# A four-layer graph network on one core: layer 0 moved beside the scatter of the edge records, with the edge counts taken from its own matmuls

## The chip, the cores and the metric

The kernel runs on one core of a Trainium2 chip. The core has a tensor engine (PE, whose weight loads are shown as PEld), a vector engine (VectorE, shown as DVE), a scalar engine (ScalarE, shown as ACT), GpSimd (shown as POOL) and SyncE (SP), which only issues DMAs here. ACT and POOL issue DMAs too. Each engine works off its own instructions in order and waits on semaphores. The metric is device time of one execution in microseconds (us); smaller is better.

## The reference, cut to what matters

There are 12500 nodes with 16 features and 412500 edges (200000 random pairs in both directions, and a loop at each node), sorted by target `dst`. Four layers follow one another, each with a residual and a layer norm over the 16 features:

```python
x = _layernorm(x + _L0_gnn_ref(x, src, dst, edge_type_8, ...))      # one 16x16 matrix per edge type, then a gated unit
x = _layernorm(x + _L1_gnn_ref(x, edge_attr_16, ..., src, dst))     # a matrix from each edge's 16 attributes
x = _layernorm(x + _L2_gnn_ref(x, ..., edge_index, edge_type_8))    # twice: sums over edge types, each divided by its count
x = _layernorm(x + _L3_gnn_ref(x, edge_index, ...))                 # reflections, weighted by 1/sqrt(degree) of both ends
```

Layer 0 sums `emb[type(e)] @ x[src(e)]` over the edges `e` of each target. Layer 2 needs, for every target and every one of 8 types, `1 / max(count, 1)`, where the count is the number of edges of that type into the target. Layer 3 needs `1 / sqrt(degree)`, where a node's degree counts it as source and as target.

## The kernel before, in words

**Places.** `find_places` (L804) computes for each edge its place in a table `rb` in DRAM. The table has 100 blocks of 125 targets (and one spare block); a block holds 39 tiles of 128 edges, grouped in 13 cells by the block of the source: `cells_of` (L794) gives a cell 3 tiles, or 2 or 4. A record is 20 floats: node number of the target within its block, the same of the source, the low three bits of the source's block, the type, and the 16 attributes. Unused places hold codes that match nothing. `find_places` also sets a flag if the edges are not sorted or a cell overflows, and then `general_path` runs instead of `sorted_path`; with this input it doesn't.

**Scatter and counts.** `sorted_path` (L930) first turns the codes by PE transposes and DVE arithmetic (L1102 to L1134). Then, in chunks of 32 tiles (`CT`), SP loads the attributes into a buffer `rec` (L1153), ACT writes the four codes beside them (L1155), and POOL issues one indirect DMA for each of the 3223 tiles of 128 edges, called a put here (L1158). The puts are declared free of dependencies on each other. In the same loop each tile is counted: DVE makes four one-hot rows by comparisons (L1147), and PE multiplies them to `cnt_ps` and `deg_ps` (L1172, L1176). The code orders PE, DVE, ACT and SP by hand there (`manual_schedule`: each engine issues in the order in which the program is written); POOL's order is the scheduler's. At the end the counts become `inv`, a tile in SBUF of all inverse counts, and `dis`, the inverse roots of the degrees (L1181 to L1194).

**Layers.** After that the node features are loaded and turned, and `table`, three bf16 parts of them, is made (n0, L1401 to L1409). `by_type` runs layer 0 (called e0, L1410) and, later, both halves of layer 2 (e2a, L1543, and e2b, L1548); between them stands layer 1 (e1, L1455), and layer 3 (e3) is last. Each of these five runs over all 1300 cells in a written-out software pipeline (`Layer.run`, L1292): in step i the work is `prepare`, delayed functions, then stage `rows` of cell i, `products` of cell i-1, and `sums` of cell i-2. In `by_type`:

- `rows`: three bf16 matmuls gather the source rows (L1265); DVE masks them with the low bits (L1267); POOL makes a one-hot row of targets for each tile (L1276).
- `products`: PE folds the masked rows (L1346); DVE multiplies by the type's one-hot `w8` (L1348).
- `sums`: PE adds a block's messages by type and target into `acc` (L1372). With `mean` (e2a, e2b) the block's inverse counts are spread by DVE (L1363), turned by PE (L1365) and copied by ACT (L1369), and multiply the sums (L1382). Later one matmul applies the types' matrices (L1388).

`start_of` (L1306) places the preparation: the record load of block d+2 in cell 3 of block d (L1222), the turning of its codes in cell 6, only in e0 (L1229 to L1233), the broadcast loads of block d+1 in cell 0 (L1237, L1239), and the one-hots of its source columns in cells 8 to 10 (L1246).

Of the kernel before, what the change touches and what calls it, by code (L numbers as in the profile page):

```python
# [8 lines left out]
F32 = mybir.dt.float32  # L9
# [8 lines left out]
P = 128  # L18
D = 16
R = 8  # L20
# [22 lines left out]
CT = 32  # L43
ENG = mybir.EngineType
# [759 lines left out]
def find_places(tc, a, rb, addr_d, flag):  # L804
# [3 lines left out]
    with tc.tile_pool(name="nat", bufs=1) as nat, tc.tile_pool(name="natp", bufs=1, space=PSUM) as psum:  # L808
# [46 lines left out]
        bads = small("bads", [P, 2])  # L855
        nc.vector.scalar_tensor_tensor(
            junk, prv_i, 1.0, dst_i, op0=OP.mult, op1=OP.is_gt, accum_out=bads[:, 0:1]
        )
        keep = big("keep")
# [63 lines left out]
        bad_ps = psum.tile([1, 2], F32, name="bad_ps")  # L923
# [7 lines left out]
def sorted_path(ctx: ExitStack, tc: tile.TileContext, a: dict, out: bass.AP, rb: bass.AP, addr_d: bass.AP):  # L931
# [43 lines left out]

    def column(name, w, j=0):
        to = const.tile([P, 1], F32, name=name)
        nc.sync.dma_start(to, w[:, j : j + 1])
        return to
# [34 lines left out]
    inv = state.tile([P, NDB, R], F32, name="inv")  # L1014
# [72 lines left out]

    with tc.tile_pool(name="sort", bufs=1) as sort, tc.tile_pool(name="sortp", bufs=1, space=PSUM) as psum:
        at = sort.tile([P, NT], I32, name="at")
        js, ds = sort.tile([P, NT], F32, name="js"), sort.tile([P, NT], F32, name="ds")  # L1090
        jd, dr = sort.tile([P, NT], F32, name="jd"), sort.tile([P, NT], F32, name="dr")
        lo, ty = sort.tile([P, NT], BF16, name="lo"), sort.tile([P, NT], BF16, name="ty")

        def by_tile(to, rows):

            for q in range(0, NQ, 4):
                n = min(4, NQ - q)
                tp = psum.tile([P, 4, P], F32, name="tp", bufs=2)
                for k in range(n):
                    nc.tensor.transpose(tp[:, k, :], rows[:, q + k, :], ident)  # L1100
                w = min(n * P, NT - q * P)
                nc.scalar.copy(to[:, q * P : q * P + w], tp.rearrange("p b f -> p (b f)")[:, :w])  # L1102

        with tc.tile_pool(name="code", bufs=1) as work:
            rows = work.tile([P, NQ, P], F32, name="rows_f")
            nc.vector.memset(rows, 0.0)
            whole = NT // P
            nc.sync.dma_start(
                rows[:, :whole, :], addr_d[: whole * P * P].rearrange("(q r i) -> r q i", r=P, i=P)
            )  # L1110
            nc.scalar.dma_start(
                rows[: NT - whole * P, whole, :], addr_d[whole * P * P :].rearrange("(r i) -> r i", i=P)
            )
            by_tile(at, rows)
            for to, name in ((js, "src"), (jd, "dst"), (ty, "edge_type_8")):
                rows_i = work.tile([P, NQ, P], I32, name="rows_i")
                nc.sync.dma_start(rows_i, a[name].rearrange("(q r i) -> r q i", r=P, i=P))
                rows = work.tile([P, NQ, P], F32, name="rows_f")
                nc.vector.tensor_copy(rows, rows_i)
                by_tile(to, rows)  # L1120
            q = work.tile([P, NT], I32, name="q")
            fix = work.tile([P, NT], F32, name="fix")
            for j, b in ((js, ds), (jd, dr)):
                nc.vector.tensor_scalar(q, j, 1049.0, None, op0=OP.mult)
                nc.vector.tensor_scalar(q, q, 17, None, op0=OP.logical_shift_right)
                nc.vector.tensor_copy(b, q)
                nc.vector.scalar_tensor_tensor(j, b, -float(NB), j, op0=OP.mult, op1=OP.add)
                nc.vector.tensor_scalar(fix, j, 0.0, None, op0=OP.is_lt)
                nc.vector.tensor_sub(b, b, fix)
                nc.vector.scalar_tensor_tensor(j, fix, float(NB), j, op0=OP.mult, op1=OP.add)  # L1130
# [860 lines left out]
```

## Time and profile before

| | |
|---|---|
| time, median of 3 runs (lowest to highest) | 22925.8 us (22896.29 to 22970.97) |
| the profiled execution: its own time | 22977.63 us |
| its span | 22975.7 us |
| mean granted PE clock | 0.919 |
| places and code columns, up to the first put | 0 to 594 us |
| scatter (puts), counting beside it up to 3229 us | 594 to 5266 us |
| layer 0 (n0 and e0) | 5266 to 7985 us |
| layer 1 (e1) | 8056 to 11530 us |
| e2a, then e2b | 11530 to 14139, 14139 to 16754 us |
| layer 3 and output | 16754 to 22975 us |

The profile's page begins with the busy time of each engine, then cuts the span into 40 equal slices (one digit each, tenths of the slice in which the engine was busy; PEclk is the clock that was granted to PE, in tenths of full speed). The chain that ended last is followed back from the last instruction, and its shares are given by engine and line. Groups of instructions show the engine, the operation, output and inputs by the program's names, shapes, the number, busy time and mean duration in ns, and the idle time before them with what ended it. A table of windows gives for each stretch its length, the busy time (and instructions) of each engine, the granted clock, the DMA share and GB/s. A timeline line has start, duration, engine, line and operation. A line of waits has the engine and line that waited, what it waited for, the total in us, the number and the longest.

### The profile page before, as it was taken

The numbers are of one execution on the slowest core, as the hardware profiler recorded it, in microseconds if no ns is written. First come the engines' busy times: TensorE is split into PE (matmuls) and PEld (weight loads), VectorE is DVE, ScalarE is ACT, GpSimd is POOL, SyncE is SP. The second block draws the span as 40 slices with busy tenths as digits, with TensorE's granted clock in tenths as the row PEclk, the third lists the DMA queues.
The fourth block names the chain that finished last, engine by engine and source line by source line (L and its number), as shares of the span: only waits on it lengthen the run. The fifth ranks groups of instructions, "written<-read, shape, count | busy, mean of one in ns | idle before, by whom it ended". The sixth has DMA issues, their size and how long they took to land.

```text
span 22975.7 us, 392949 instructions
## 1 busy us (share of the span) xinstructions
PE 18801.4 (82%) x144828; PEld 16753.0 (73%) x144830; DVE 15165.8 (66%) x35158; ACT 2307.5 (10%) x8260; POOL 16182.6 (70%) x22749
## 2 busy tenths in 40 slices
PE   0666640007999999999989999999989999999998
PEld 0444430006888878888888888888879999999998
DVE  7999960004656666666666666666657777777776
ACT  0000000000000001111100000000022222222222
POOL 2788877777988866666689998999934545554444
PEclk9999985558989999999999999999979999999998
DMA  2100011112323244444433332333323333333333
GB/s 94 13 12 12 12 13 15 15 15 75 92 82 86 78 143 139 141 142 142 131 86 91 90 92 81 90 92 90 92 75 97 106 97 105 104 102 103 99 104 80
DMA packets 1173120, 1910.62 MB, mean 83 GB/s; under 512 B 578330, under 2 KB 962721, under 8 KB 1094017
## 3 DMA queue, kind: packets, MB, share of 16 engines
q1 hardware_dynamic: 1050430, 1830.86, 28.4%
q0 software_dynamic: 103136, 33.21, 1.0%
q8 instruction: 1154, 18.91, 0.4%
q10 hardware_dynamic: 17627, 21.31, 0.3%
q14 instruction: 773, 6.33, 0.1%
HBM read 1557.01 MB, written 327.89 MB: 82 GB/s over the span
## 4 chain that ended last, share of the span: by engine, by line
PE 63%; POOL 19%; DMA 6%; issue 5%; DVE 5%; another core or an unknown queue 0%; ACT 0%; SPq 0%; POOLq 0%; ACTq 0%; DVEq 0%
POOL rb L1158 15%; PE g L1265 12%; PE acc L1372 10%; PE acc L1488 8%; PE x L1346 8%; DMA rec<-rb 5%; PE acc_s L1835 4%; PE hid_ps L1720 4%; POOL target L1276 4%; PE acc_s L1828 3%; PE side L1728 3%; PE x L1471 3%; PE edge_ps L1689 3%; PE acc_s L1619 1%; DMA rb<-rec,at 1%
## 5 line engine op out<-in xcount | busy, mean ns | idle before, releaser
L1276 POOL TENSOR_SCALAR target<-iota_f,rec 128x125 f32<-128x125 f32 x15600 | 9376.8, 623 | 2079.9 <-PE acc L1488 904.0
L1267 DVE SCALAR_TENSOR_TENSOR masked<-lo,part_lo,g 128x384 f32<-128x384 uint8 (+2 forms) x6500 | 3985.0, 613 | 3612.2 <-PE g L1265 3524.3
L1816 POOL TENSOR_SCALAR from_s<-iota_f,js_e 128x125 f32<-128x125 f32 x3900 | 2954.1, 773 | 3233.3 <-PE acc_s L1835 2991.8
L1265 PE MATMUL g<-oh,table 125*128 125x384 bf16 (+2 forms) x19500 | 4359.2, 332 | 169.6 <-DVE oh L1246 103.9
L1158 POOL DMA_INDIRECT rb<-rec,at x3223 | 3690.4, 1145 | 1074.5 <-issue 982.0
L1372 PE MATMUL acc<-target,pr 128*128 128x125 f32 x23400 | 3632.2, 292 | 0.0
L1346 PEld LDWEIGHTS x<-fold,masked 128*128 128x128 f32 x23400 | 3197.0, 196 | 280.1 <-issue 22.1
L1372 PEld LDWEIGHTS acc<-target,pr 128*128 128x128 f32 x23400 | 3012.6, 197 | 0.4
L1346 PE MATMUL x<-fold,masked 128*128 128x16 f32 x23400 | 2948.2, 252 | 0.0
L1265 PEld LDWEIGHTS <-table 125*128 125x128 bf16 x19500 | 1970.8, 106 | 880.7 <-issue 212.6
L1172 PE MATMUL cnt_ps<-in_col,in_row 128*125 128x400 bf16 x6446 | 1607.7, 330 | 915.4 <-DVE in_col L1147 915.4
L1348 DVE TENSOR_TENSOR pr<-x,w 128x384 f32<-128x384 f32 (+2 forms) x3900 | 2170.7, 557 | 134.0 <-PE x L1346 108.0
L1488 PE MATMUL acc<-pr,target 128*125 128x272 f32 x7800 | 2106.6, 406 | 0.0
L1172 PEld LDWEIGHTS <-in_row 128*125 128x125 bf16 x6446 | 857.5, 133 | 1262.2 <-issue 643.5
L1045 PE MATMUL tp<-ident,x_rows 125*128 125x125 f32 x13 | 5.9, 465 | 2052.1 <-DMA x_rows<-in_x 2050.1
L1488 PEld LDWEIGHTS acc<-pr,target 128*125 128x125 f32 x7800 | 1364.8, 188 | 216.9 <-issue 0.3
L1045 PEld LDWEIGHTS tp<-ident,x_rows 125*128 125x128 f32 x13 | 2.4, 182 | 2055.6 <-issue 2043.0
L1474 DVE TENSOR_TENSOR pr<-x,rec 128x768 f32<-128x768 f32 (+2 forms) x1300 | 1244.8, 958 | 257.1 <-ACT pr L1473 251.9
L1147 DVE TENSOR_SCALAR in_col<-iota_h,dr 128x800 bf16<-128x800 f16 x3223 | 1322.9, 410 | 0.0
L1835 PE MATMUL acc_s<-placed,from_s 128*125 128x128 f32 x7800 | 1249.1, 299 | 53.8 <-DVE acc_s L1833 51.4
L1192 DVE RECIPROCAL dis<-root 128x104 f32<-128x104 f32 x1 | 0.8, 803 | 1921.7 <-ACT root L1191 1921.7
L1720 PE MATMUL hid_ps<-x_t,w_h 96*128 96x128 f32 (+2 forms) x7800 | 1188.1, 292 | 0.0
(303 smaller groups left out, 25808.5 us busy)
## 6 DMA issues: line engine op xcount, KB each, us to landing
hi<-hi_d SPq DMA_DIRECT2D x400, 1218.8 KB
lo<-lo_d SPq DMA_DIRECT2D x500, 624.0 KB
to_d<-target SPq DMA_DIRECT2D x1108, 187.5 KB
target<-to_d SPq DMA_DIRECT2D x1108, 187.5 KB
rec<-rb SPq DMA_DIRECT2D x500, 390.0 KB
oh<-hi_d SPq DMA_DIRECT2D x100, 1218.8 KB
to_t<-jd_d SPq DMA_DIRECT2D x100, 1218.8 KB
rb<-rec,at POOLq DMA_INDIRECT x3223, 2.5
```

What stands on the lines that cost most here:

```text
L1158: put = nc.gpsimd.indirect_dma_start(out=rb, out_offset=bass.IndirectOffsetOnAxis(ap=at[:, t : t + 1], axis=0), in_=rec[:, k, :], in_offse ...
L1172: nc.tensor.matmul(cnt_ps[:NB, h, :NC2], in_row, in_col[:, h * NC2 : (h + 1) * NC2], start=False, stop=False, skip_group_check=True,)
L1265: nc.tensor.matmul(g[:, :w], tab[:NB, s, k, :], self.oh[d][:NB, cols], start=k == 0, stop=k == 2)
L1267: nc.vector.scalar_tensor_tensor(m[:, :w], self.lo[d][:, cols], part_lo, g[:, :w], op0=OP.is_equal, op1=OP.mult)
L1276: nc.gpsimd.tensor_scalar(oh[:, k, :], iota_f[:, :NB], self.rec[d][:, t + k, code : code + 1], None, op0=OP.is_equal)
L1346: nc.tensor.matmul(x[:, k, :D], m[:, k * P : (k + 1) * P], fold, start=True, stop=True)
L1348: nc.vector.tensor_tensor(pr[:, :n], x[:, :n, None, :D].to_broadcast([P, n, R, D]), layer.w8[d][:, t : t + n, :, None].to_broadcast([P, n, ...
L1372: nc.tensor.matmul(acc[:, :NB], pr[:, k].rearrange("p r f -> p (r f)"), oh[:, k, :], start=t + k == 0, stop=t + k == TB - 1,)
L1488: nc.tensor.matmul(acc[:NB, :WE], oh[:, k, :], pr[:, k, :], start=t + k == 0, stop=t + k == TB - 1)
L1720: nc.tensor.matmul(ps[:, k * P : (k + 1) * P], w_h[rows, k, :], x_t[rows], start=True, stop=True)
L1816: nc.gpsimd.tensor_scalar(oh[:, k, :], iota_f[:, :NB], js_e[d][:, t + k : t + k + 1], None, op0=OP.is_equal)
L1835: nc.tensor.matmul(acc_s[:NB, s // 4, s % 4, :], oh[:, k, :], placed[:, k].rearrange("p l f -> p (l f)"), start=False, stop=False, skip_gr ...
```

## The change

Layer 0 runs inside the scatter's loop. The diff, cut to its core:

```diff
+EB = 4125
+WAYS = 8
+SLACK = 2048
...
+        nc.gpsimd.iota(q, pattern=[[1, NT]], base=0, channel_multiplier=NT)
+        nc.vector.tensor_copy(x1, q)
+        nc.vector.scalar_tensor_tensor(x1, d, -float(EB), x1, op0=OP.mult, op1=OP.add)
+        nc.vector.tensor_scalar(x1, x1, float(EB + SLACK), None, op0=OP.is_ge)
+        nc.vector.tensor_reduce(bads[:, 2:3], x1, AX.X, OP.add)
...
-                for t in range(t0, t0 + n):
-                    in_row = one_hot("in_row", jd[:, t : t + 1], NB)
-                    in_col = one_hot("in_col", dr[:, t : t + 1], NDB * R)
-                    out_row = one_hot("out_row", js[:, t : t + 1], NB)
-                    out_col = one_hot("out_col", ds[:, t : t + 1], NDB)
...
-            nc.sync.dma_start(self.rec[d], rb_v[d])
+            load = nc.sync.dma_start(self.rec[d], rb_v[d])
+            tc.add_to_no_dep_group("records", getattr(load, "ins", load))
...
-            tp = self.psum.tile([P, 4, P], F32, name="codes_t", bufs=1)
+            tp = self.psum.tile([P, 512], F32, name="g", bufs=2).rearrange("p (b c) -> p b c", b=4)
...
+                for k in range(n):
+                    rec = layer.rec[d][:, t + k, :]
+                    nc.vector.tensor_scalar(oh[:, k, :], iota_f[:, :NB], rec[:, 0:1], None, op0=OP.is_equal)
+                    nc.scalar.activation(away[:, k, :], iota_f[:, :NB], AF.Abs, bias=rec[:, 1:2], scale=-1.0)
+                source = work.tile([P, 4, NB], BF16, name="source", bufs=4)
+                nc.scalar.activation(source[:, :n], away[:, :n], AF.Relu, bias=1.0, scale=-1.0)
+                for _ in range(2):
+                    nc.tensor.matmul(
+                        deg_ps[:, P:], zeros[:, :P], zeros[:, P:], start=False, stop=False, skip_group_check=True
+                    )
...
-                if mean and s == NS - 3:
...
+                if mean and s == 2:
...
-                    nc.scalar.copy(state_["inv", d], ps[:, :NB])
+                    nc.sync.dma_start(state_["inv", d], inv_d[d])
...
+                    if first:
...
+                        nc.tensor.matmul(
+                            acc[:R, P : P + NB], layer.w8[d][:, t + k, :], oh[:, k, :].bitcast(BF16)[:, 1::2],
+                            start=False, stop=t + k == TB - 1, skip_group_check=True,
+                        )
+                        nc.tensor.matmul(
+                            deg_ps[:NB, s * LO : (s + 1) * LO], source[:, k, :], layer.lo8[d][:, t + k, :],
+                            start=False, stop=False, skip_group_check=True,
+                        )
...
+                def count():
+                    nc.tensor.matmul(
+                        deg_ps[:NB, d : d + 1], cnt, ones8, start=False, stop=False, skip_group_check=True
+                    )
+                    ps = psum.tile([P, 4, 32], F32, name="x", bufs=2).rearrange("p k c -> p (k c)")
+                    nc.tensor.matmul(ps[:, :NB], spread8, cnt, start=True, stop=True)
+                    inv = work.tile([P, NB], F32, name="inv_t", bufs=2)
+                    nc.vector.tensor_scalar(inv, ps[:, :NB], 1.0, None, op0=OP.max)
+                    nc.vector.reciprocal(inv, inv)
+                    nc.sync.dma_start(inv_d[d], inv)
...
+            def fed(layer, steps):
...
+                chunk(0)
+                chunk(1)
+                i = 0
+                for t in range(NT + WAYS):
+                    if t % CT == 0:
+                        chunk(t // CT + 2)
+                    put(t)
+                    while i < len(all_cells) and (EB * max(3.0, 3 + (i - 3) / NS) + SLACK) / P + WAYS < t:
+                        next(steps)
+                        i += 1
+                for _ in steps:
+                    pass
```

In words:

- `fed` writes the program so that after put t those steps of e0 stand whose records can't lie behind put t-8, as long as no edge of a block stands more than 2048 edges behind its mean place. `find_places` checks that in addition (four DVE passes and an iota). A block takes 4125/128 = 32.2 puts. Eight puts to the spare block are added at the end. The attributes and codes of a chunk are asked for two chunks ahead, in four buffers instead of three.
- The separate counting is gone, with the columns that only it used. In e0 each tile gets two thin matmuls more: `w8` times the targets' one-hots, which counts edges by type and target into a free part of `acc`, and the sources' one-hots times the one-hots of the low bits (`lo8`), which counts degrees. The sources' one-hots come from ACT (Abs, then Relu). Two matmuls of zeros with 384 columns stand in each cell.
- In e0 the targets' one-hots are made by DVE instead of POOL; in the other layers POOL keeps them. `w8` is bf16 in all `by_type` layers.
- After each block of e0 its counts are spread over the features by PE, limited to 1 and inverted by DVE, and stored in DRAM (`inv_d`, 64 KB). e2a and e2b load that in cell 2 of a block instead of copying, turning and copying from `inv`.
- The load and turning of the node features and `table` (n0) stand ahead of the code columns, since e0 needs them from the start.

## Prediction

> **What bounds the kernel now.** I first read the slices of the span on the page: the tensor engine (PE) stands idle in slices 7 to 9 while GpSimd (POOL) works on, and everything behind them is a row of nines.
>
> ```profile
> PE   0666640007999999999989999999989999999998
> ...
> DVE  7999960004656666666666666666657777777776
> ...
> POOL 2788877777988866666689998999934545554444
> PEclk9999985558989999999999999999979999999998
> ...
> POOL rb L1158 15%; PE g L1265 12%; PE acc L1372 10%; PE acc L1488 8%; PE x L1346 8%; DMA rec<-rb 5%; PE acc_s L1835 4%; PE hid_ps L1720 4%; POOL target L1276 4%; PE acc_s L1828 3%; PE side L1728 3%; PE x L1471 3%; PE edge_ps L1689 3%; PE acc_s L1619 1%; DMA rb<-rec,at 1%
> ```
>
> The last line is from the chain that ended last: 15% of the span is the scatter, L1158. Its 3223 puts are one chain on POOL from 594.0 to 5265.5 us. Then I cut the span at the stage borders (first instructions of each stage, from the per-line view): busy time of PE, weight load, DVE, ACT, POOL, then the granted clock.
>
> ```profile
> 594.00:3175.00 2581.00, 1711.61 (x9460) 1260.70 (x9458) 2581.00 (x12612) 29.99 (x196) 2100.67 (x1577) 1.00 0.10 12
> 3175.00:5266.00 2091.00, 36.84 (x206) 27.03 (x204) 63.44 (x275) 31.59 (x198) 1589.31 (x1647) 0.51 0.12 14
> 5266.00:7984.00 2718.00, 2586.70 (x20011) 2355.74 (x20011) 1702.80 (x3003) 92.67 (x417) 2349.12 (x3901) 0.94 0.32 87
> ...
> 11530.00:14139.00 2609.00, 2486.25 (x19921) 2281.42 (x19921) 1750.98 (x3207) 37.37 (x123) 2358.22 (x3900) 0.98 0.33 89
> ```
>
> Row 1: scatter beside counting, DVE full. Row 2: counting is done, scatter alone, PE at half clock with nothing to do. Row 3: layer 0 (e0), bounded by PE (95% busy). Row 4: e2a, the same. So 4672 us hang on POOL, then 2718 us on PE, one after the other. The put itself is seen at two prices; timeline of POOL in both stretches:
>
> ```profile
> 4000.17 0.96 POOL L1158 DMA_INDIRECT rb<-rec,at  x1 [0.30 <-issue]
> ...
> 2001.70 1.34 POOL L1158 DMA_INDIRECT rb<-rec,at  x1 [0.30 <-issue]
> ```
>
> Busy 0.96 us and 0.30 between: one put per 1.263 us beside an idle DVE (3.79 us for three at 4000.17); 1.34 and 0.30, one per 1.637 us (2581/1577) beside a DVE that does nothing but L1147's comparisons. That difference of 0.374 us is the disputed price.
>
> **The change, part by part.**
>
> *1. First put (+34 us).* Loading x and making the table now comes ahead: 27 us (5267.8, first x load issued, to 5295.0, first record load issued). Four more DVE passes over 128x3223 in the check (1.8, 3.5, 1.8, 3.5 us by the rows of L1126, L1127, L1128, L1129) and an iota, 3.3 us (L951: 0.81 us for 800 columns, times 4): 14. Two passes go with the counting's columns (L1129, L1134 of dst, 3.5 each): -7. First put at 594 + 34 = 628.
>
> *2. The puts.* 3223, and 8 to the spare block: 3231 at a price r. It lies between 1.263 and 1.637 by the two rows. DVE's work per block of targets in e0: masked 7.97 us (L1267, 3985.0/500), pr 7.24 (L1348, 2170.7/300), the 39 target one-hots that leave POOL for DVE, 39 x 0.2 = 7.8 (L1147 starts one of 125 columns every 0.16; L953, 128 columns of f32, lasts 0.21), column one-hots 3 x 0.70 (L1246), w8 and lo8 1.0 (L1253), maximum and reciprocal 1.2 (L1192: 0.80 for 104 columns): 27.3 us. Of these 11.1 (one-hots, maximum, reciprocal) resemble L1147's. A block is 4125 edges, 32.2 puts, about 43.7 us. I take the surcharge as proportional: 0.374 x 11.1/43.7 = 0.095, r = 1.358, 3231 x 1.358 = 4388 us. Last put at 5016. I keep both ends: 4081 to 5289.
>
> *3. Does e0 fit below it?* PE: today (7984 - 5326)/100 = 26.6 us a block, of which 1.3 waits. Added: 39 counting matmuls of 125 columns and 39 degree matmuls of 8, and 26 of zeros with 384 (two a cell). The nearest rows, in layer 3:
>
> ```profile
> 20011.42 0.29 PE L1691 MATMUL edge_ps<-x_parts,to_t 125*128 125x96 bf16 x3
> 20011.55 0.23 PE L1696 MATMUL side<-dis_tab,oh 125*128 125x24 bf16 x3
> 20011.63 0.81 PE L1828 MATMUL acc_s<-msg,target 128*125 128x16 f32 x6
> ```
>
> Starts tell the price: three of 96 columns in 0.13 us, three of 24 in 0.08. So 0.06 and 0.03 each: 3.5 us; those of zeros 0.163 as in L1265 (0.49 for three): 4.2. Together 33 us. DVE 27.3. ACT: per cell three activations of 0.26 (L1380, 128x125) and one of at most 0.58 (L1722, 384 columns), 17.7 a block, with codes, counts and record columns 21. All are under 43.7, so the puts stay the bound, and the counting's 12612 DVE instructions (2581 us, row 1) vanish. Target one-hots on POOL, 24.3 us a block, would have stood in the puts' queue; moved, they don't. On SP each block's record load waits for the put before it, and behind it stand column stores and broadcasts (1219 and 624 KB), the inverse's store and the next chunk's attributes. Chunks are asked for two ahead, 64 puts or 87 us; a block's queue is at most 44 us late if PE keeps pace. If that cover went, POOL would wait for ACT and SP: rival A.
>
> *4. What is late next.* The program lets a block start some 3.5 blocks behind its last possible edge: 35 cells remain after the last put, 35 x 33/13 = 89 us, plus load and broadcast of the last block: 115 (89 to 230 if half-clocked). e0 ends at 5016 + 115 = 5131; layer 0's gates today start at 7985 (L1421). Gain 2854.
>
> *5. e2a and e2b.* The turned inverse (L1363, L1365, L1369) becomes a 64 KB load.
>
> ```profile
> PEld x L1365 <- PE x L1346: 85.4, 86, 1.0
> PE x L1365 <- DVE by_f L1363: 79.5, 86, 0.9
> ```
>
> PE waits 0.94 us a block for the copy (188.1/200 over both layers) and issues two f32 passes, 0.22: 200 x 1.16 = 232 us. POOL's targets (three start in 1.75 us, 22.8 a block) and the load, asked for ten cells ahead, are not later. Ends: 0 (something else is late at once) to 290 (35 short half-clock stretches go too). I take 230, since PE is busy 95% around that wait.
>
> *6. bf16 w8, a shared PSUM ring for the transposed codes:* 0, the first lies beside PE, the second can at worst hold PE for ACT's two further copies of 0.26 a block (L1232): 0 to +52, inside the tail's and r's bounds, since e0 is not the bound.
>
> **Sum** against the profiled execution (22977.6, span 22975.7): 22977.6 - 2854 - 230 = 19894. That execution lies 52 us above the median 22925.8; with the same cut the median becomes 19842, say **19850**.
>
> [...]
>
> [...] PE around a wait of 1.47 us for records in e0:
>
> ```profile
> 5660.00:5690.70 30.70, 29.68 (x244) 1.00 0.35 97
> 5690.70:5694.20 3.50, 2.03 (x17) 1.00 0.03 10
> 5694.20:5718.10 23.90, 23.90 (x106) 0.50 0.27 80
> 5718.10:5745.00 26.90, 26.90 (x222) 1.00 0.23 62
> ```
>
> One such wait brought 23.9 us at half clock, and 106 instructions where 190 would go. [...] By the row PE, ready after 33 of 43.7 us, will wait, drop, fall behind, not wait, and recover: it needs a mean clock of 0.76 and lags less than the 87 us of cover. Counting ran at clock 1.00 with PE 66% busy (row 1), with gaps of 0.3 us.
>
> **Rivals.**
> A. *PE stays at half clock.* For: the row above. Against: row 1, and a PE that is behind has no gaps. 66 us a block; e0 would end at 628 + 164 (121 puts ahead of the first cell) + 6600 = 7392, 2261 later: 22,100. 13%.
> B. *No overlap:* each record load waits for all puts. For: one tensor, rb, is written and read, and only puts are declared free of each other. Against: the wait is for puts issued before the load. Then 628 + 3231 x 1.263 + 3300 = 8009, and with e2's gain 22,720. 5%.
> C. *Slower: the put's price explodes.* If a put that loses to DVE waits for a whole train of three one-hots, twice, it costs 1.263 + 2 x 0.6 = 2.46 us, e0 ends at 628 + 7948 + 115 = 8691, time 23,400. It decides from r = (7985 + 230 - 628 - 115)/3231 = 2.31. For: DVE did slow puts. Against: a DVE without a gap cost only 0.374. 5%.
>
> **Numbers.** Forecast 77%: own range 19,450 (r 1.263, e2 290, short tail) to 20,980 (r 1.637, e2 0). Range 19,450 to 21,300, which takes in blocks of up to some 57 us from A. The measurement tells 0.3% (69 us) from no change. Faster 0.94, same 0.01 (B with a small extra wait), slower 0.05.
>
> **What would show it.** Puts from about 628 at 1.30 to 1.45 us apart throughout, e0's matmuls from about 800, layer 0's gates near 5130; PE 75 to 95% busy there at a clock above 0.75; no wait of PE for an inverse in e2, blocks of 25 us. Wrong if POOL waits for ACT's record columns by more than some us per chunk (A), if e0 starts behind the last put (B), or if puts are over 1.64 apart (C).

## The result and the profile after

The changed kernel takes 24,767.0 us (median of 4 executions, 24,735.9 to 24,807.6), the kernel before 22,931.4 (22,896.3 to 22,971.0): a ratio of 1.0801 with a 95% interval of 1.0777 to 1.0825. The forecast was 19,850. The profiled execution took 24,807.6 us (span 24,805.8).

| stage border (us from the span's start) | before | forecast | after |
|---|---|---|---|
| first put | 594.0 | 628 | 621.9 |
| last put | 5265.5 | 5016 | 9830.2 |
| layer 0's gates (its gated unit's first product, behind all its sums) | 7985.3 | 5131 | 10183.6 |
| from the gates to the end | 14990.4 | 14760 | 14622.2 |

So everything behind layer 0 gained 368 us, and layer 0 with its scatter, which was to gain 2854, lost 2198.

The page of the changed kernel, first the slices (busy tenths, granted clock), then the chain that ended last, then the put's row in the costliest groups (busy us, mean ns of one, idle before and its releaser):

```profile
PE   0478777776777777999999999999998999999998
...
POOL 2433333323333332366666899999993554545544
PEclk9555555556565555899999999999997999999998
...
PE 79%; another core or an unknown queue 10%; DVE 5%; issue 3%; POOL 1%; DMA 1%; ACT 0%; SPq 0%; ACTq 0%; DVEq 0%; POOLq 0%
...
L1454 POOL DMA_INDIRECT rb<-rec,at x3223 | 3102.2, 963 | 6159.0 <-ACT rec L1445 4244.4
```

TensorE now works in the scatter, but at a clock of 0.5 to 0.6 from slice 2 to slice 16. GpSimd, which was to set the pace, is three tenths busy. A put still lasts 0.96 us, so its price didn't rise; GpSimd stands idle for 6159 us, mostly until ScalarE has filled the columns of a chunk of 32 tiles. And 10% of the chain, some 2480 us, has no releaser that the profile knows. That last item is the odd one, so I cut one period into windows: busy PE, weight load, DVE, ACT, POOL, then the clock, DMA share, GB/s.

```profile
622.00:9830.00 9208.00, 6725.46 (x28912) 4753.62 (x28912) 2460.72 (x6765) 1841.36 (x5764) 3108.80 (x3230) 0.55 0.13 32
4017.00:4039.00 22.00, 21.66 (x84) 15.25 (x83) 4.83 (x14) 4.85 (x16) 16.33 (x17) 0.50 0.05 7
4039.00:4063.00 24.00, 3.97 (x14) 2.34 (x14) 1.07 (x2) 0.11 (x1) 14.40 (x15) 0.50 0.05 7
4063.00:4110.00 47.00, 46.37 (x186) 32.91 (x186) 17.83 (x50) 12.56 (x38) 0.00 (x0) 0.50 0.22 57
9860.00:9960.00 100.00, 100.00 (x412) 71.62 (x412) 34.11 (x94) 25.18 (x76) 0.00 (x0) 0.52 0.08 25
13700.00:18600.00 4900.00, 4823.08 (x39476) 4436.11 (x39476) 3478.99 (x6231) 29.48 (x61) 4715.92 (x7800) 0.99 0.37 97
```

Row 2: a burst of 32 puts begins at 4017.6 and TensorE works beside it. Row 3: in the second half of the same burst TensorE issues 14 matmuls in 24 us, VectorE 2 instructions, ScalarE 1. Row 4: the burst is over, GpSimd waits, TensorE is full, at half clock. Row 5: all puts are done and TensorE is 100% busy without one gap, and still at 0.52. Row 6 lies over layer 2's two passes; from the first of their sums to the last they take 4832 us instead of 5178. Inside row 3, in the timeline:

```profile
4043.68 0.29 PEld L1306 LDWEIGHTS acc<-target,pr 128*128 128x128 f32 x1 [1.72 <-issue]
4044.16 0.96 POOL L1454 DMA_INDIRECT rb<-rec,at  x1 [0.31 <-issue]
4045.08 0.37 PE L1306 MATMUL acc<-target,pr 128*128 128x125 f32 x1 [2.63 <-issue]
...
4045.43 0.96 POOL L1454 DMA_INDIRECT rb<-rec,at  x1 [0.30 <-issue]
4045.78 0.37 PE L1306 MATMUL acc<-target,pr 128*128 128x125 f32 x1 [0.33 <-issue]
4046.48 0.08 PEld L1313 LDWEIGHTS <-w 128*8 128x8 bf16 x1 [1.11 <-issue]
...
4061.90 0.29 DVE L1350 TENSOR_SCALAR inv_t<-x 128x125 f32<-128x125 f32 x1 [25.36 <-remote]
```

TensorE waits for "issue", that is for nothing that the profile shows, and its instructions start 0.70 or 1.40 us apart (4043.68, 4045.08, 4045.78, 4046.48). From layer 0's first matmul to the last put, 794 matmuls start more than 0.6 us behind the one before, 2601 us in all; the kernel before has no such interval while it counts. In the median of 94 bursts of 32 puts the first long interval begins 18 us behind the first put. So two things need a cause: this stall, and a half clock that a full TensorE doesn't leave.

In e2, e5 and e8, which have two products with zeros per cell, two executions differ by 2 to 4%, with the mean clock (e2: 25,665 us at 0.812, 24,712 at 0.849), so both times are given, and the profile with its gates and block times is of the first, longer one.

### The profile page after: what moved, and what is told of

Same layout as the page of the kernel before. It is cut to its first block, busy times and chain, and to the rows that moved or that the text cites. A ratio compares the mean times of both kernels' runs of the same rounds, so it can differ in the third digit from the quotient of the medians.

```text
span 24805.8 us, 382593 instructions
## 1 busy us (share of the span) xinstructions
PE 21351.2 (86%) x145557; PEld 17953.5 (72%) x145557; DVE 13400.1 (54%) x26263; ACT 4061.7 (16%) x13360; POOL 13268.0 (53%) x18859
## 4 chain that ended last, share of the span: by engine, by line
PE 79%; another core or an unknown queue 10%; DVE 5%; issue 3%; POOL 1%; DMA 1%; ACT 0%; SPq 0%; ACTq 0%; DVEq 0%; POOLq 0%
PE acc L1306 16%; PE g L1178 14%; PE x L1286 11%; PE acc L1557 8%; PE acc_s L1904 4%; PE hid_ps L1789 4%; PE acc_s L1897 3%; PE x L1540 3%; PE side L1797 3%; PE edge_ps L1758 3%; PE deg_ps L1317 3%; PE acc L1313 3%; PE deg_ps L1277 3%; PE acc_s L1688 1%
## 5 line engine op out<-in xcount | busy, mean ns | idle before, releaser
L1189 POOL TENSOR_SCALAR target<-iota_f,rec 128x125 f32<-128x125 f32 x11700 | 7028.6, 623 | 1719.5 <-PE acc L1557 905.0
L1454 POOL DMA_INDIRECT rb<-rec,at x3223 | 3102.2, 963 | 6159.0 <-ACT rec L1445 4244.4
L1306 PE MATMUL acc<-target,pr 128*128 128x125 f32 x23400 | 5098.6, 341 | 853.2 <-issue 539.7
L1286 PEld LDWEIGHTS x<-fold,masked 128*128 128x128 f32 x23400 | 3806.9, 227 | 1078.7 <-issue 580.0
L1306 PEld LDWEIGHTS acc<-target,pr 128*128 128x128 f32 x23400 | 3867.4, 228 | 881.0 <-issue 551.8
L1275 ACT ACTIVATE source<-away 128x375 bf16<-128x375 bf16 (+2 forms) x1300 | 672.6, 517 | 3923.3 <-PE deg_ps L1317 2515.6
L1273 ACT ACTIVATE away<-iota_f,rec 128x125 bf16<-128x125 f32 x3900 | 1258.0, 387 | 0.0
L1758 PEld LDWEIGHTS edge_ps<-fold,masked 128*128 128x128 f32 x7800 | 1091.4, 200 | 96.8 <-DVE ends L1804 7.9
L1317 PE MATMUL deg_ps<-lo,source 128*125 128x8 bf16 x3900 | 992.1, 254 | 144.7 <-issue 144.6
L1540 PEld LDWEIGHTS x<-fold,masked 128*128 128x128 f32 x7800 | 1038.9, 192 | 88.7 <-DVE masked L1180 0.6
L1897 PE MATMUL acc_s<-msg,target 128*125 128x16 f32 x7800 | 1086.9, 265 | 0.0
```

What stands on the lines that cost most here:

```text
L1189: nc.gpsimd.tensor_scalar(oh[:, k, :], iota_f[:, :NB], self.rec[d][:, t + k, code : code + 1], None, op0=OP.is_equal)
L1286: nc.tensor.matmul(x[:, k, :D], m[:, k * P : (k + 1) * P], fold, start=True, stop=True)
L1306: nc.tensor.matmul(acc[:, :NB], pr[:, k].rearrange("p r f -> p (r f)"), oh[:, k, :], start=t + k == 0, stop=t + k == TB - 1, skip_group_ch ...
L1454: to_place = nc.gpsimd.indirect_dma_start(out=rb, out_offset=bass.IndirectOffsetOnAxis(ap=to, axis=0), in_=recs[t // CT][:, t % CT, :], in ...
L1758: nc.tensor.matmul(edge_ps[:, k, :D], m[:, k * P : (k + 1) * P], fold, start=True, stop=True)
```

## The experiments

Theory when they began: puts 1.263 us apart stall the other engines (the kernel before ran puts beside work only at 1.637), and layer 0's new mix of products doesn't bring TensorE back to full clock. Block times below are the distances of the inverse counts' reciprocals, one per block.

**e1, puts spaced out, first try.**

```diff
                 tc.add_to_no_dep_group("records", to_place)
+                nc.gpsimd.tensor_scalar(spare, iota_f[:, :NB], 1.0, None, op0=OP.is_equal)
```

> After each put GpSimd does one comparison of 128x125 into a spare tile that nobody reads (0.59 to 0.62 us by the rows of its kind), so puts stand about 1.88 us apart instead of 1.263; nothing else is changed. Theory 'close puts stall the engines': the 20 to 27 us in each burst in which TensorE issues one instruction per 0.70 or 1.40 us come from puts 1.263 us apart (beside puts 1.637 us apart the kernel before ran without them). They go, and a block takes the 60 to 66 us of TensorE at half clock, or the 32.2 x 1.88 = 60.6 us of its puts, whichever is longer: layer 0's gates at about 7,300 to 7,800 us instead of 10,183, the whole kernel at 21,900 to 22,500 us. Rival 'the products themselves stall whatever the spacing': the bursts are 60 us long instead of 39 and the stall stays in them: gates at 10,200 us or later, 24,800 us or more. The clock stays at 0.50 to 0.60 in either.

Measured: 24,887 and 25,059 us, gates at 10,263.9, but a median of 1.263 us from put to put. The comparisons were placed into GpSimd's waits, ahead of the puts (252 of them before the first put, which came at 766.0), so nothing was spaced. It tells nothing on the theory; it shows that GpSimd has that time to spare.

**e2, all puts first.**

```diff
-                    while i < len(all_cells) and (EB * max(3.0, 3 + (i - 3) / NS) + SLACK) / P + WAYS < t:
+                    while False:
```

> All 3,231 puts come first, and layer 0's steps, thin products and all, only behind the last put: no overlap. Last put at about 622 + 3,231 x 1.263 = 4,700 us in either theory. Theory 'the mix of products holds TensorE at half clock by itself': a block takes 60 to 66 us without any put beside it, the gates come at 10,900 to 11,400 us and the kernel at about 25,500 to 26,000 us. Rival 'the gaps of the bursts bring the clock down, and alone it recovers': clock near 0.9, 27 to 35 us a block, gates at 7,500 to 8,250 us, kernel at 22,100 to 22,900 us.

Measured: 25,665 and 24,712 us, last put at 4706.9, gates at 10,992.2, no interval over 0.6 us while puts run (TensorE has nothing to do). Windows without any put:

```profile
4841.20:5016.80 175.60, 175.60 (x975) 128.78 (x973) 81.12 (x228) 60.30 (x182) 0.00 (x0) 0.76 0.14 42
8000.00:9000.00 1000.00, 1000.00 (x4108) 715.29 (x4107) 351.61 (x960) 255.02 (x766) 0.00 (x0) 0.52 0.09 32
8230.60:8302.10 71.50, 71.50 (x287) 51.02 (x285) 24.94 (x69) 17.93 (x55) 0.00 (x0) 0.50 0.10 34
8302.30:8305.50 3.20, 3.20 (x23) 2.38 (x23) 1.07 (x4) 1.17 (x4) 0.00 (x0) 1.00 0.00 0
```

TensorE is 100% busy in all of them. Thirty-four blocks at full clock take 43.9 us each, those at half clock 75 to 78. It holds either clock for several blocks, and from 8000 us to the end of layer 0 the mean is 0.52: in each block of 75 us the clock comes back once, for some 3.4 us, and falls again (rows 3 and 4). So the mix alone keeps the half clock, without a stall; the rival (gaps of the bursts) falls as the only cause. The shorter execution, 24,712 us, lies between the two cases, with a mean clock of 0.849 instead of 0.812. With this mix 1000 us without a gap (row 2, mean clock 0.52) didn't bring the full clock back to stay: being busy wasn't enough.

**e3, thin products left out.**

```diff
-                        nc.tensor.matmul(acc[:R, P : P + NB], layer.w8[d][:, t + k, :], ...
-                        nc.tensor.matmul(deg_ps[:NB, s * LO : (s + 1) * LO], source[:, k, :], ...
-                nc.scalar.copy(cnt, acc[:R, P : P + NB])
+                nc.scalar.copy(cnt, acc[:R, :NB])
```

> The thin products are left out (those that count edges per target and relation and those that count outgoing edges), so the counts, and what is divided by them, are not the reference's; puts, one-hots and the two products with zeros stay. Theory 'the thin products hold the clock down': TensorE comes back to full clock between the bursts, a block takes about 28 us of TensorE plus the stall of 20 to 27 us: 50 to 55 us, gates at 5,900 to 6,300 us, kernel at 20,500 to 20,900 us. Rival 'the bursts' stall holds it down': half clock stays, a block loses only the thin products' own time (26 of some 100 us): 75 to 80 us, gates at 8,200 to 8,800 us, kernel at 22,800 to 23,400 us. The stall within the bursts stays in either if the puts make it, and gets smaller if TensorE's many small instructions do.

Measured: 22,161 us, ratio 0.9651 (0.9566 to 0.9735), gates at 7499.6: between the two. The clock does come back to 1.00 between the bursts (mean 0.69), but the stall grew to 3115 us: a faster TensorE just meets it sooner. Five blocks at full clock take 29.2 us (a sixth, the last of layer 0, takes 20.9), so the thin products cost 43.9 - 29.2 = 14.7 us a block. Starts at full clock show how: without them the two passes of an f32 product follow 0.11 us apart, but for the first of a cell (0.19); with a thin pair behind each (e2) the f32 product takes 0.40 and the pair 0.23, 0.62 per tile instead of some 0.25.

**e4, six products with zeros per cell instead of two.** (`for _ in range(2)` becomes `range(6)` at L1276.)

> Six products of 384 columns with zeros in each cell instead of two. Theory 'TensorE streams too small a share of the time to be given the full clock': with four more (0.16 us each at full clock) the clock returns to 1.00 outside the stalls, a block takes 33 + 8 us and the stall of 20 to 27: 61 to 68 us, gates at 7,000 to 7,500 us, kernel at 21,600 to 22,100 us. Rival 'streaming does not matter, the stall holds it down': they are paid at half clock, 4 x 0.32 us x 13 cells = 17 us more per block, gates at about 11,850 us, kernel at 26,400 us.

Measured: 24,104 us, 1.0497 (1.0423 to 1.0571), gates at 9499.5. Windows of 10 us in one period:

```profile
4110.00:4120.00 10.00, 10.00 (x39) 6.08 (x38) 3.52 (x10) 2.77 (x8) 0.00 (x0) 0.50 0.00 0
4120.00:4130.00 10.00, 10.00 (x67) 7.55 (x66) 5.20 (x14) 2.48 (x7) 0.00 (x0) 0.94 0.09 24
4130.00:4140.00 10.00, 10.00 (x71) 7.16 (x71) 4.49 (x12) 3.19 (x9) 0.00 (x0) 1.00 0.52 169
...
4160.00:4170.00 10.00, 4.38 (x17) 3.06 (x16) 0.56 (x1) 0.00 (x0) 7.56 (x9) 0.67 0.06 8
4170.00:4180.00 10.00, 2.26 (x7) 1.41 (x6) 0.00 (x0) 0.00 (x0) 7.56 (x9) 0.50 0.06 8
```

More streaming does bring the clock back, some 20 us behind each stall, and the next burst takes it away. It moves the gates by only 684 us, since puts and products still take turns: 86.2 us a block. The clock theory holds; its expected size fails: a block's work takes 52.2 us at full clock, not 41, and the stall is 31 us (3077 us in 100 blocks), not 20 to 27.

**e5, puts spaced out with GpSimd's order held as written** (GpSimd joins the engines of `manual_schedule`; else e1).

> The spaced-out puts once more, now with GpSimd's order held as written: in e1 the comparisons were moved into the waits between the bursts, so that its puts still stood 1.263 us apart. Each put is followed by one comparison of 128x125 into a tile that nobody reads: 1.88 us from put to put. Theory 'close puts stall the engines': no instruction of TensorE waits 0.70 or 1.40 us any more, a block takes 60 to 66 us (TensorE at half clock, or 32.2 puts of 1.88), gates at 7,300 to 7,800 us, kernel at 21,900 to 22,500 us. Rival 'puts and layer 0's products shut each other out at any spacing': the stall lasts as long as the burst, which is now 60 us: a block at 120 us, gates at about 12,500 us, kernel at 27,000 us.

Measured: 22,077 and 21,657 us, gates at 7439.9. Timeline of GpSimd, then one window of all engines:

```profile
3000.11 1.05 POOL L1456 DMA_INDIRECT rb<-rec,at  x1 [0.18 <-issue]
3001.20 0.56 POOL L1464 TENSOR_SCALAR spare<-iota_f 128x125 f32<-128x125 f32 x1
3001.94 1.05 POOL L1456 DMA_INDIRECT rb<-rec,at  x1 [0.18 <-issue]
```

```profile
1000.00:6500.00 5500.00, 5404.99 (x26081) 3913.21 (x26081) 2288.69 (x6098) 1655.26 (x5176) 4564.99 (x5568) 0.64 0.20 47
```

At 1.83 us a put TensorE is 98% busy; 12 long intervals are left of 794, none of them 0.70 or 1.40 us (the shortest is 5.0). Work added to GpSimd brought the gates some 2740 us forward. What is left is the clock: 65.4 us a block on average, but 43.9 in the blocks at full clock (27 of 99, the last of which is shorter). The second execution, 21,657 us, is faster than expected; its mean clock is 0.878 instead of 0.858.

**e6, loads that depend on nothing beside the puts.** (A stage: `put(t)`, a fill of one element, and for TensorE alone for instance `nc.tensor.matmul(pz[:, :384], zeros[:, :P], zeros[:, :384], ...)` twice.)

> All puts come before layer 0, as in e2; beside them run, 128 puts to a stage, loads that depend on nothing of the puts: on TensorE alone bf16 products of 384 columns, f32 products of 16 columns, f32 products of 125 columns, thin bf16 pairs, a mix of all; the mix with one, two and three comparisons of 128x125 on GpSimd behind each put; VectorE alone, ScalarE alone, all three; VectorE and TensorE as the kernel before counted; a chain that goes to and fro between TensorE and VectorE; the mix once in two and once in four puts. Each stage begins when all engines have ended the one before, and most of the loads run once more behind the puts as a measure. (A tiny fill stands behind each put to hold the order.) Theory 'close puts stall the engines': the steps of 0.70 and 1.40 us show in every stage whose TensorE load is large and whose puts stand 1.3 us apart, and are gone with one comparison between (1.9 us). Rival 'only what waits for other engines is stalled': nothing is stalled but the chain and the stages with VectorE's and TensorE's work tied together. Rival 'f32 products are stalled (several passes each)': f32 stages alone are stalled, bf16 ones run at their own speed. Rival 'the puts stall nothing, the loads of records do': no stage shows such steps.

| stage | median us from put to put | matmuls while puts run, of those asked | intervals over 0.6 us |
|---|---|---|---|
| bf16, 384 columns | 1.266 | 164 of 256 | 106 |
| f32, 16 columns | 1.266 | 188 of 512 | 99 |
| f32, 125 columns | 1.266 | 190 of 512 | 104 |
| thin bf16 pairs | 1.266 | 191 of 512 | 98 |
| mix | 1.266 | 194 of 1024 | 94 |
| mix, one comparison per put | 1.864 | 998 of 1024 | 0 |
| TensorE's share of the old counting | 1.267 | 164 of 384 | 115 |
| the old counting, VectorE too | 1.638 while VectorE works | all 384 | 0 |

(f32 products count twice, once for each pass; idle time at a stage's end is left out.) Windows of the first, the fifth and the sixth row, of VectorE alone, ScalarE alone and the last row:

```profile
794.30:977.40 183.10, 63.95 (x165) 17.14 (x166) 0.12 (x2) 2.60 (x18) 133.98 (x256) 0.53 0.11 13
1710.60:1889.20 178.60, 56.10 (x195) 36.56 (x194) 0.00 (x0) 2.19 (x16) 133.82 (x255) 0.50 0.10 12
2089.60:2327.60 238.00, 238.00 (x1000) 175.22 (x997) 0.00 (x0) 2.16 (x17) 214.83 (x384) 0.50 0.07 9
3045.20:3225.30 180.10, 0.83 (x4) 0.72 (x4) 97.58 (x289) 2.39 (x17) 135.37 (x256) 0.50 0.11 13
3255.10:3431.80 176.70, 0.46 (x3) 0.35 (x2) 0.00 (x0) 93.40 (x302) 133.88 (x256) 0.50 0.10 12
4413.40:4599.10 185.70, 71.89 (x389) 53.17 (x389) 105.05 (x515) 2.54 (x19) 157.62 (x258) 0.78 0.11 13
```

Close puts stall every kind of product, though nothing there waits for anything, and VectorE and ScalarE too (289 and 288 of 384 instructions; the window of ScalarE also holds copies of columns). All three rivals fall. The last two rows of the table are the key to the kernel before: its counting would have been stalled as well, had VectorE's one-hots not slowed the puts to 1.64 us. Two stages without any load, where GpSimd's own fill alone stood behind each put, averaged 1.36 and 1.38 us a put at a median of 1.266, since fills came late; puts without a fill (e2) averaged 1.265. So the fill is held like any other instruction.

Behind the puts the same program runs the loads once more, alone: bf16 products of 384 columns, f32 of 16, f32 of 125, thin pairs, and the mix:

```profile
6767.20:6785.80 18.60, 18.60 (x116) 11.16 (x114) 0.00 (x0) 0.00 (x0) 0.00 (x0) 1.00 0.00 1
6791.10:6836.90 45.80, 45.80 (x217) 45.80 (x216) 0.00 (x0) 0.00 (x0) 0.00 (x0) 0.50 0.00 1
6842.40:6868.90 26.50, 26.50 (x240) 26.50 (x239) 0.00 (x0) 0.00 (x0) 0.00 (x0) 1.00 0.01 1
6873.10:6919.00 45.90, 45.90 (x235) 30.74 (x234) 0.00 (x0) 0.00 (x0) 0.00 (x0) 0.50 0.00 1
6920.00:7042.00 122.00, 121.62 (x512) 89.66 (x511) 0.25 (x2) 0.31 (x2) 0.11 (x1) 0.50 0.00 1
```

TensorE is full in all five, and the clock goes by the kind of product: 1.00 with the wide ones (rows 1 and 3), 0.50 with f32 products of 16 columns, thin pairs and the mix. Rows 2 and 4 began at full clock and lost it after 4.2 and 2.7 us. So layer 0's fold (f32, 16 columns) and its thin products are both of the kind that does not hold the clock; with the fold but without the thin products the kernel before kept it at 0.94 in layer 0.

**e7, the inverse counts in DRAM alone, in the kernel before.**

```diff
-                if mean and s == NS - 3:
+                if first and s == NS - 3:
...
+                    nc.sync.dma_start(inv_d[d], inv_t)
+                if mean and s == 2:
+                    nc.sync.dma_start(state_["inv", d], inv_d[d])
```

> The kernel before with one part of the change alone: each block's inverse counts are spread by copy, product and copy once, in layer 0, and stored; layer 2's two passes load them instead of making them anew. In the changed kernel the stages behind layer 0's gates took 14,622 us instead of 14,990: 368 us, some 180 per pass. One pass's work is added in layer 0, whose TensorE is 95% busy. If that work costs there what it cost in layer 2: -368 + 180 = 22,740 us. If it is hidden in layer 0: 22,560 us. If layer 2 does not gain from the load: 22,930 us or more.

Measured: 24,169 us, 1.0546 (1.0517 to 1.0576): slower by far. Only the third case's number allows that, and its condition doesn't hold: behind the gates it gained 321 us, but the gates came at 9463.8. Waits in layer 0 (us, times, longest):

```profile
SPq L1370 <- ACT inv_t L1369: 2192.7, 99, 41.6
```

```profile
PE codes_t L1230 <- DMA rec<-rb: 438.1, 94, 6.5
```

SyncE waits for the copy that it is to store, and the next block's load of records stands behind it. TensorE then waits 4.7 us a block for the records, and loses the clock (0.65 to 0.71 instead of 0.92 to 0.96). In the changed kernel SyncE waits for the inverse as well (2698 us between 2000 and 8000), but its record loads come early enough: behind layer 0's start TensorE waits 9.6 us for them in all, and not at all between 1000 and 5500 in e12.

**e11, the same with the store on ScalarE's queue** (`nc.scalar.dma_start(inv_d[d], inv_t)`).

> As e7, but the store of the inverse counts stands on ScalarE's queue behind the copy that makes it. In e7 SyncE waited 1,035 us in 2,000 (24.8 us each) for that copy, with the next block's load of records queued behind; TensorE then waited 5 us a block for the records, and the clock in layer 0 fell from 0.95 to 0.70: 4,200 us instead of 2,720. Theory 'the store in front of the loads did it': TensorE's wait and the clock are the kernel before's again, layer 0 takes 2,720 to 2,890 us, layer 2 keeps its 321 us: kernel at 22,580 to 22,760 us. Rival 'the added product in layer 0 does it': 24,100 us as in e7.

Measured: 22,605 us, 0.9858 (0.9826 to 0.9890), gates at 7964.6, as the theory has it. (The 24.8 us named above is the longest of e7's waits; their mean is 1035.3/49 = 21.1.) The wait for records:

```profile
PE codes_t L1230 <- DMA rec<-rb: 4.3, 9, 0.8
```

The choice of the queue was worth 1,560 us, and this part of the change by itself gains 1.4% (1.1 to 1.7).

**e8, a narrower comparison** (`spare[:, :40]`, `iota_f[:, :40]`, else e5).

> As e5, with a comparison of 128x40 instead of 128x125 behind each put: 1.45 us from put to put by the rows of e5 and e6 (1.266 with a fill of 0.09 us, 1.83 with 0.57 us). Theory 'something that takes about 1.40 us per put is shared with all engines' instructions' (32 puts of 1.263 us and the 6 us until the engines go on make 1.40 us a put; the steps in the stall are 0.70 and 1.40 us): at 1.45 us nothing piles up, no step of 0.70 or 1.40 us shows, and the rest is e5's: blocks of 44 us at full and 75 us at half clock, gates at 7,000 to 7,700 us, kernel at 21,400 to 22,100 us. Rival 'the threshold lies nearer 1.55 us': part of the stall is back, gates beyond 8,000 us, kernel beyond 22,400 us.

Measured: 21,707 and 21,111 us, gates at 7032.2; four intervals over 0.6 us, none of them 0.70 or 1.40. But the puts stood 1.609 us apart (median), not 1.45, since a comparison on GpSimd shrank far less than its columns (0.56 us for 128x125 in e5, still 0.26 to 0.35 for 128x8 in e12), so the threshold wasn't tried.

**e9 and e10, spaced puts (comparison of 128x64) with four and six products with zeros.**

> Puts spaced by a comparison of 128x64 (about 1.53 us), and four products with zeros per cell instead of two. Theory 'two separate things: close puts stall, and too thin a mix does not come back to full clock': without the stall and with more streaming the clock stays at 1.00; a block takes 48 us of TensorE (43.9 at full clock with two, 13 x 2 x 0.16 more) or 32.2 x 1.53 = 49.3 us of puts: gates at 5,900 to 6,100 us, kernel at 20,500 to 20,750 us. Rival 'four are too few': blocks at half clock of 75 + 8 us for a large part, gates at 7,000 to 9,000 us, kernel at 21,600 to 23,600 us.

> As e9 with six products with zeros per cell. Theory: the clock stays at 1.00 as it did in e4 between the stalls; a block takes the 52.2 us that e4's blocks took at full clock: gates at 6,150 to 6,300 us, kernel at 20,750 to 20,950 us. It costs 4 us a block more than e9 if four hold the clock, and beats e9 if they do not. Rival 'the clock falls for a reason that more streaming does not heal': clock under 0.9 and gates beyond 6,800 us.

Measured: e9 20,905 us, 0.9116 (0.9085 to 0.9148), gates at 6256.5, clock about 0.9; e10 20,884 us, 0.9108 (0.9078 to 0.9138), gates at 6266.5, clock 0.97. Both take 53.9 us a block. The two causes are separate: zeros alone (e4) bring the gates 684 us forward, spacing alone (e5) 2744, both together some 3920. In both runs the puts set the pace (32.2 x 1.672 = 53.8; GpSimd waits for no other engine for more than 2 us in all between 1000 and 5500). In e9 TensorE waits 176 us there for records and loses the clock in half of the blocks; in e10 it has more work (63 blocks at full clock take 52.6 us), waits 34 us and keeps the clock. e10 is within what was expected; e9 came 155 us above it, because a put cost 1.672 us, not 1.53.

**e12, comparison of 128x8, five products with zeros.**

> In e9 the puts stood 1.672 us apart (median) and 32.2 of them, 53.8 us, made a block's mean of 53.9: GpSimd was the bound, and TensorE, with 48 us of work, waited for records and lost the clock in half of the blocks. Here the comparison behind each put is 128x8, and five products with zeros stand in a cell: about 1.52 us a put (0.063 us less from 64 to 40 columns, so some 0.15 us less from 64 to 8), 49 us a block, and 50.2 us of TensorE at full clock. Theory 'something that takes about 1.40 us per put is shared': no step of 0.70 or 1.40 us, TensorE is the bound and keeps the clock, 50 to 52 us a block, gates at 5,950 to 6,150 us, kernel at 20,550 to 20,800 us. Rival 'the threshold lies above 1.52 us': such steps are back, GpSimd bursts and waits, gates beyond 6,400 us, kernel beyond 21,000 us.

Measured: 20,747 us, 0.9050 (0.9017 to 0.9084), puts at 1.516 us, gates at 6063.1, 52.1 us a block, no such steps.

```profile
PE   0499999999999999999999999999899999999998
...
PEclk9799999999989999999999999999899999999998
```

As expected, TensorE is the bound now: 100% busy from 1000 to 5500 us, with 50.2 us in a block at full clock. It is the fastest version, 9.5% below the kernel before, and all that it has over the changed kernel is a comparison per put that nobody reads, GpSimd's order held, and three more products with zeros per cell.

**e13, where the threshold lies, and whether rows matter.** (e6's stages with a fill of w columns behind each put, and puts of the first 64 or 32 rows.)

> All puts ahead of layer 0 again, 128 to a stage, and beside each put four independent products on TensorE (two of bf16 with 384 columns, two of f32 with 16). Behind each put stands a fill of 1, 24, 48, 72, 96, 128 or 192 columns: by the fills of 0.09 us (one element) and 0.73 us (128x606) some 1.27, 1.30, 1.33, 1.35, 1.38, 1.41 and 1.48 us from put to put. Then puts of 64 and of 32 rows only with the smallest fill, and of 64 rows with the fill of 96 columns; these leave out the other rows of their tiles, so edges are missing in the output. Theory 'about 1.40 us per put of 128 rows is shared with all engines' instructions': steps of 0.70 and 1.40 us in the stages up to 1.35 us, fewer at 1.38, none at 1.41 and 1.48. Rival 'the share grows bit by bit': TensorE's products per put rise slowly over the stages and no stage is sharp. With 64 or 32 rows: if the shared thing is paid by rows or by what the rows' transfers signal, those stages show no such steps even where their puts stand closer together; if it is paid by put, they show them as before.

| fill, rows | median us from put to put | mean | matmuls per put (6 asked) | intervals over 0.6 us |
|---|---|---|---|---|
| 1, 128 | 1.263 | 1.393 | 1.6 | 96 |
| 96, 128 | 1.322 | 1.387 | 1.6 | 92 |
| 128, 128 | 1.349 | 1.404 | 2.0 | 97 |
| 192, 128 | 1.402 | 1.404 | 2.2 | 106 |
| 1, 64 | 1.202 | 1.399 | 1.4 | 106 |
| 1, 32 | 1.169 | 1.396 | 1.4 | 95 |
| 96, 64 | 1.267 | 1.408 | 1.9 | 84 |

The fills were shorter than I had worked out, so no stage passed 1.40. But the mean settles it better than the threshold would have: however close the puts are issued, GpSimd's fills are held back in steps until the puts average 1.39 to 1.41 us, and with 32 rows as with 128. It isn't paid by row; each put brought 32 packets in all of these stages, so put and packet aren't told apart. The stage at 1.402 still shows the steps and e12 at 1.516 doesn't, so the limit lies between. (Fills of 24, 48 and 72 columns gave the same as the first row.)

## Why the prediction was wrong

*Step 1, first put:* right, 621.9 for 628.

*Step 2, price of a put:* it is the lower end, 1.263. Layer 0's comparisons did not cost the 0.095 us that I took: in e12 a put takes 1.516 us before layer 0 begins and 1.516 beside it, where in e6 the old one-hots made 1.64 of 1.27. Layer 0's are f32 with 125 columns, L1147's were 16-bit with 100 to 800 and kept VectorE full; which of these differences counts, no run shows. That is small; what failed is what I took the price for. I asked only what the other engines do to a put, and not what puts at that distance do to the other engines. The rows were on the table: row 1 of my windows has work beside puts, at 1.637 us; row 2 has 1.263, beside idle engines. No row showed both, and I added them.

*Step 3, "does e0 fit below it?":* this is the step that failed, in three terms. (a) "33 us" of TensorE is 43.9 at full clock; the thin products cost 14.7 a block where I had 3.5, and the rest of the sum, 29.5, was right (29.2). I had taken 0.06 and 0.03 us from layer 3's products, which have other shapes; e6's thin pairs take 0.30 us at full clock even alone, and between f32 products some 0.38. That alone fills the 43.7 us of a block. (b) PE that falls behind will "not wait, and recover": e2 shows it without gaps and at a mean of 0.52 to the end; 75 us a block, more than rival A's 66. (c) "Chunks are asked for two ahead" was no cover against that: ScalarE copies a chunk's columns behind layer 0's steps, so when TensorE lags, GpSimd waits (2858 us between 2000 and 8000, up to 65.5), and then issues 32 puts in one burst that stalls TensorE. Puts and products take turns. The sign that I had named for rival A was the one that appeared; the burst and its stall were in none of my cases, so the range, which went to 21,300, missed by far. Rival C had the right side for a wrong reason: 2.85 us a put (9208/3230), but no put cost more.

*Where the 5052 us between 5131 and 10,183.6 went:* spacing the puts brings the gates to 7439.9 (2744 less; the clock rises from 0.55 to 0.64 with it), the clock and a closer spacing to 6063.1 (1377 less). How these two share is rough, since e5's other execution was 420 us shorter. Of the remaining 932 most are TensorE's: 50.2 us a block with five products with zeros instead of 43.7 makes 650, and the tail 210 (325 for 115).

*Step 4, the tail:* not reached as meant; from the last put to the gates 353 us passed in the changed kernel and 325 in e12, for my 115 (89 to 230).

*Step 5, layer 2:* mechanism right, size too small: 368 us behind the gates, of them 345 in layer 2, for 230 (0 to 290); e7 and e11 gained 321 and 335 behind the gates. TensorE's 186 us of waits for the inverse are gone as forecast, and the clock in layer 2 rose from 0.979 to 0.996, worth some 90 us by an estimate (215 and 38 us at half clock), which the forecast had only in its upper end, at 58. *Step 6:* nothing in the trace points to it; it wasn't tried by itself.

What stays open is why the engines are held until some 1.40 us per put have passed (1.39 to 1.41 in e13). In the kernel before the trace holds 16.0 signals per put (a semaphore's updates at its landing) while the puts run alone, from 3175 to 5266 us, and 15.9 beside the counting. While puts are close and other instructions run, it holds only 3.7 in the changed kernel, 2.4 to 3.7 in e13's stages and 3.8 and 4.1 in e6's two stages with the fill alone; in e2, at 1.265 us a put without a fill, it holds 15.6, in e12 15.9, but in e5, where nothing stalls, 11.2. Every execution here is recorded, so no run separates the recording from the transfers themselves. Whether an execution without recording would stall is not shown.

## What to carry to other kernels

If the profile shows two things only apart, it does not show them together: before laying work beside a stream of transfers, look for a row in which that stream runs at the speed it will have, with work beside it. A producer at its highest rate can be the wrong setting; here GpSimd was made slower by 20% a put and the kernel 16% faster (24,767 to 20,747, with the clock's part). And a wait in the middle of a store queue (e7) or a thin mix of products (e2) was paid twice on TensorE: once as itself (4.7 us a block in e7, 14.7 in e2 by e3's difference) and once as the lower clock behind it (0.65 to 0.71 instead of 0.92 to 0.96 in e7, blocks of 75 us instead of 43.9 in e2).

## What the runs showed of the hardware

- Beside indirect puts on GpSimd, 32 packets each, at medians of 1.169 to 1.402 us from put to put, some 1.3 to 2.2 matmuls went through per put, of each kind that was tried (e6, e13), in the changed kernel in steps of 0.70 or 1.40 us; VectorE and ScalarE were held too (289 and 288 of 384 instructions, e6), and GpSimd's own fills: with a fill behind each, the puts beside products averaged 1.39 to 1.41 us (e13). Puts without a fill ran at 1.265 (e2) and 1.27 (2091 us for 1647 in the kernel before). At 1.516 us (e12) no such steps showed, and TensorE was 100% busy from 1000 to 5500 us. All of this was seen in recorded executions.
- TensorE 100% busy stayed at a mean clock of 0.52 for 1000 us and more with a mix of f32 and thin products (e2); alone, f32 products of 16 columns and thin bf16 pairs stood at 0.50, f32 products of 125 columns and bf16 products of 384 at 1.00 (e6). Two to four products of 384 columns more per cell kept layer 0 at 0.89 to 0.97 (e9, e10, e12).
- f32 comparisons of 125 columns on VectorE left the price of a put alone (1.516 us with and without, e12); 16-bit ones of 100 to 800 columns that filled VectorE raised it from 1.27 to 1.64 us (e6).
- A thin bf16 pair between f32 products costs some 0.38 us per tile at full clock: 0.23 for itself, the rest because the f32 passes go from 0.11 to 0.20 us each (e2, e3). Thin pairs among their own kind take 0.30 us (two starts of 0.15, e6).
